# Second moments of attention keys from channel products on VectorE and GpSimd, in place of squared sums from TensorE and ScalarE

## The chip, the cores and the metric

The kernel runs on one core of one Trainium2 chip. The metric is the device time in microseconds (us) from launch to end; lower is better. Three runs of the kernel before gave 4068.22, 4074.77 and 4081.95 us, so the median is 4074.77. One more execution was taken with the hardware profiler.

The engines are called here as the profile calls them: PE is TensorE (matmuls), PEld its loading of weights, DVE is VectorE, ACT is ScalarE, POOL is GpSimd, SP is SyncE, which issues most of the DMAs. Everything is computed in float32.

## The reference, cut to what matters

The network has a convolution layer, then an attention layer, then a feed-forward layer on the upper half of the tokens. The images are 4 x 256 channels x 56 x 56, so the attention sees 4 batches of N = 3136 tokens of 256 channels, with 8 heads of 32 channels. Only the attention is touched by the change:

```python
NUM_HEADS = 8
C_SHIFT = 5.0
qkv = x @ qkv_w.T + qkv_b
q, k, v = (qkv[:, :, 0], qkv[:, :, 1], qkv[:, :, 2])
scores = jnp.einsum('bnhd,bmhd->bhnm', q, k) * scale
t = jnp.square(scores + C_SHIFT)
attn = t / jnp.sum(t, axis=-1, keepdims=True)
out = jnp.einsum('bhnm,bmhd->bnhd', attn, v)
return out @ proj_w.T + proj_b
```

The weight of a key is the square of a shifted score, so it is a polynomial of degree two in the key. The sum over all keys can therefore be taken before the queries are known. What is needed of the keys of one head is the sum over tokens of v times each product of two channels k_i k_j (the second moments), of v times k_i, and of v alone, and for the divisor the same sums without v.

## The kernel before, in words

The program has three parts, one after the other: `conv_layer`, the attention in `attn_ffn_layers`, and the feed-forward layer at the end of `attn_ffn_layers`.

**How the attention is staged.** For each of the 4 images b, `keys(b, 0)` and `keys(b, 1)` (line 1000) gather the sums over keys for the two groups of four heads; after each, `coefficients(b, g)` (line 1089) turns the sums into the weights of the queries' features; then `queries(b)` (line 1179) goes over the tokens again in 7 chunks of 448. I call the two runs of `keys` of an image its key stages. The loop that sets this order is at lines 1438 to 1448.

**One token tile of a key stage.** There are NT = 25 tiles of 128 tokens (the last has 64). For tile m, in the order in which they are written:

- `features(m)` (line 1035): four matmuls (one for each head, 32 rows each) multiply the transposed keys `kT` by the constant `pairs`, whose columns each have ones at two channels. The result `pf`, 496 columns a head, is k_i + k_j for all pairs i < j. ACT squares it into `phi` (line 1048), which has two buffers; DVE sets column 496 to one (line 1046).
- `add(m - 1)` (line 1051): four matmuls add v times `phi` of the tile before into the PSUM tile `accs`; four small ones add v times the squares and the keys into `accq`; one of 128 by 129 columns adds keys times keys and keys times one, for the divisor, to `accq` as well.
- `tokens(m + 3)` (line 1009): two matmuls give keys and values `pv` of a later tile with tokens on partitions; DVE adds the bias (line 1021) to the keys in `ls` and to `v`, and squares the keys (line 1025).
- `channels(m + 2)` (line 1027): PE transposes the keys into `pk`, and DVE copies them to `kT`.

So every tile of the keys passes through PE twice before it is summed: once to be transposed, once to make the sums of pairs.

**From squared sums to products.** (k_i + k_j)^2 holds the product that is wanted and two squares. `coefficients` takes this apart. It copies the sums to SBUF, transposes them in five blocks (`pt`, `pr`), and eight matmuls with the constants `pair_to` and `rest_to` (`pc`) and six further ones (`pd`) give `cf`, the weights of the queries' pairs, and `cd`, the weights of their squares and of the queries themselves. `gram` and `line` are for the divisor.

**Work beside.** Everything that isn't in these loops is a generator in the list `later`; each `yield` of a key or query stage calls `aside()` (line 1427), which takes every one of them a step further. Four of them matter for the prediction: `divide` and `tokens_out` finish the last chunks of an image while the key stage of the next one runs (`po` on PE; `uw` and `tk` on POOL, lines 1317 and 1318); `select(b)` then finds the upper half of an image's tokens (`hit` on DVE, `pn` on PE), and at its end scatters 28 blocks of rows to the DRAM tile `us` by indirect DMAs from POOL (line 1421), two for each step; and `project` makes the queries of a chunk, with their squares on POOL (line 1152). `select` of image b runs in the key stages of image b + 1; that of the last image runs in the feed-forward layer.

**What sets the order.** The framework places semaphores and may reorder instructions of an engine. `InOrder` (line 841) wraps an engine so that its instructions keep the order in which they are written. In `attn_ffn_layers` DVE, PE, ACT and SP are wrapped (line 897). POOL isn't; its instructions there are issued through `nc.gpsimd`.

**Buffers.** `phi` has two, `ls` five (`NKV`), `v` five, `kT` four; the small PSUM tiles (`pv`, `pk`, and those of the work beside) share two of tag `sm`.

Of the kernel before, what the change touches and what calls it, by code (L numbers as in the profile page):

```python
# [7 lines left out]
F32 = mybir.dt.float32  # L8
I32 = mybir.dt.int32
AF = mybir.ActivationFunctionType  # L10
ALU = mybir.AluOpType
# [843 lines left out]
LS = 2 * DH + 1  # L855
# [3 lines left out]
def attn_ffn_layers(  # L859
    ctx: ExitStack, tc: tile.TileContext, d, xs: bass.AP, ln0: bass.AP, us, out: bass.AP  # L860
):

# [34 lines left out]
    ve, te, se, sy = (  # L897
        InOrder(tc, e) for e in (nc.vector, nc.tensor, nc.scalar, nc.sync)
# [15 lines left out]
    pair_to = const.tile([P, FB + 1, P], F32, name="pair_to")  # L914
    nc.sync.dma_start(pair_to, d["pair_to"])
    rest_to = const.tile([LS, NF + 2 * P], F32, name="rest_to")
# [26 lines left out]
    for i in range(NKV):  # L943
        ls = const.tile([P, 2 * P + 1], F32, name=f"ls{i}")
        nc.gpsimd.memset(ls[:, 2 * P :], 1.0)
        lss.append(ls)
# [53 lines left out]
    def keys(b, g):  # L1000

        xn = xns[b]
        accs = accp.tile([P, 512], F32, tag="acc", name=f"accs_{b}_{g}")
        accq = accp.tile([P, 512], F32, tag="acc", name=f"accq_{b}_{g}")
        held["sums", b, g] = accs, accq
        vs, kts = {}, {}
        size = lambda m: min(P, HW - m * P)

        def tokens(m):

            mn = size(m)
            ls = lss[m % NKV]
            v = vs[m] = kp.tile([P, P], F32, tag="v", name=f"v_{b}_{g}_{m}", bufs=5)
            p = sm.tile([P, 512], F32, tag="sm", name=f"pv_{b}_{g}_{m}")
            for c in range(2):
                te.matmul(
                    p[:mn, : 2 * P], xn[:, c, m * P : m * P + mn],
                    wqkv[:, c, C:].rearrange("p (i o) -> p i o", i=2)[:, :, g * P : (g + 1) * P],
                    start=c == 0, stop=c == 1,
                )  # L1020
            for i, to in enumerate((ls[:mn, P : 2 * P], v[:mn])):
                ve.tensor_tensor(
                    to, p[:mn, i * P : (i + 1) * P], kvb[:mn, i, g * P : (g + 1) * P], ALU.add
                )
            ve.tensor_tensor(ls[:mn, :P], ls[:mn, P : 2 * P], ls[:mn, P : 2 * P], ALU.mult)

        def channels(m):

            mn = size(m)
            p = sm.tile([P, 512], F32, tag="sm", name=f"pk_{b}_{g}_{m}")  # L1030
            te.transpose(p[:, :mn], lss[m % NKV][:mn, P : 2 * P], ident[:mn, :mn])
            kts[m] = kp.tile([P, P], F32, tag="kT", name=f"kT_{b}_{g}_{m}", bufs=4)
            ve.tensor_copy(kts[m][:, :mn], p[:, :mn])

        def features(m):
            mn = size(m)
            kT = kts.pop(m)
            p = [
                mm.tile([P, 2, 512], F32, tag="mm", name=f"pf{i}_{b}_{g}_{m}") for i in range(2)
            ]  # L1040
            for h, r in enumerate(QUARTERS):
                te.matmul(
                    p[h // 2][:mn, h % 2, :NP], kT[r, :mn], pairs[r, :NP], start=True, stop=True
                )
            phi = php.tile([P, 4, 512], F32, tag="phi", name=f"phi_{b}_{g}_{m}")
            ve.memset(phi[:mn, :, NP : NP + 1], 1.0)
            for i in range(2):
                se.activation(phi[:mn, 2 * i : 2 * i + 2, :NP], p[i][:mn, :, :NP], AF.Square)
            return phi

        def add(m, phi):
            mn = size(m)
            v, ls = vs.pop(m), lss[m % NKV]
            first, last = m == 0, m == NT - 1
            for h, r in enumerate(QUARTERS):
                te.matmul(accs[r, : NP + 1], v[:mn, r], phi[:mn, h, : NP + 1], start=first, stop=last)
            both = ls[:mn, : 2 * P].rearrange("p (i h e) -> p i h e", i=2, e=DH)
            for h, r in enumerate(QUARTERS):
                te.matmul(
                    accq[r, : 2 * DH].rearrange("p (i e) -> p i e", i=2), v[:mn, r],  # L1060
                    both[:, :, h], start=first, stop=last, skip_group_check=True,
                )

            te.matmul(
                accq[:, P : 2 * P + 1], ls[:mn, P : 2 * P], ls[:mn, P:], start=False, stop=last,
                skip_group_check=True,
            )

        tokens(0)
        tokens(1)  # L1070
        yield
        channels(0)
        tokens(2)
        yield
        channels(1)
        waiting = None
        for m in range(NT):
            phi = features(m)
            if waiting:
                add(*waiting)  # L1080
            waiting = m, phi
            if m + 3 < NT:
                tokens(m + 3)
            if m + 2 < NT:
                channels(m + 2)
            yield
        add(*waiting)

    def coefficients(b, g):
# [3 lines left out]
        st = stp.tile([P, NF + P], F32, tag="st", name=f"st_{at}")  # L1093
        ve.tensor_copy(st[:, :NP], accs[:, :NP])
        ve.tensor_copy(st[:, NF : NF + 2 * DH], accq[:, : 2 * DH])
        ve.tensor_copy(st[:, NF + 2 * DH : NF + LS], accs[:, NP : NP + 1])
        gram = cp.tile([P, P], F32, tag="gram", name=f"gram_{at}")
        ve.tensor_tensor(gram, accq[:, P : 2 * P], own.rearrange("p h e -> p (h e)"), ALU.mult)
        line = cp.tile([P, 1], F32, tag="line", name=f"line_{at}")
        ve.tensor_scalar(line, accq[:, 2 * P : 2 * P + 1], 2 * CSHIFT, None, ALU.mult)  # L1100
        held["form", b, g] = gram, line
        yield
        sums = stp.tile([P, FB + 1, P], F32, tag="sums", name=f"sums_{at}")
        kns = (P, P, P, NP - 3 * P)
        p = sm.tile([P, FB, P], F32, tag="sm", name=f"pt_{at}")
        for k, kn in enumerate(kns):
            te.transpose(p[:kn, k], st[:, k * P : k * P + kn], ident)
        ve.tensor_copy(sums[:, :3], p[:, :3])
        ve.tensor_copy(sums[: kns[3], 3], p[: kns[3], 3])
        yield  # L1110
        p = sm.tile([P, 512], F32, tag="sm", name=f"pr_{at}")
        te.transpose(p[:LS, :P], st[:, NF : NF + LS], ident)
        ve.tensor_copy(sums[:LS, FB], p[:LS, :P])
        yield
        cf = cp.tile([P, FB, 4, DH], F32, tag="cf", name=f"cf_{at}")
        p = sm.tile([P, FB, P], F32, tag="sm", name=f"pc_{at}")
        for k, kn in enumerate(kns):
            te.matmul(p[:, k], pair_to[:kn, FB], sums[:kn, k], start=True, stop=False)
            te.matmul(
                p[:, k], rest_to[:, k * P : (k + 1) * P], sums[:LS, FB], start=False, stop=True  # L1120
            )
        ve.tensor_copy(cf.rearrange("p k h e -> p k (h e)"), p)
        yield
        p = sm.tile([P, 2, P], F32, tag="sm", name=f"pd_{at}")
        for k, kn in enumerate(kns):
            te.matmul(p[:, 0], pair_to[:kn, k], sums[:kn, k], start=k == 0, stop=False)
        te.matmul(p[:, 0], rest_to[:, NF : NF + P], sums[:LS, FB], start=False, stop=True)
        te.matmul(p[:, 1], rest_to[:, NF + P :], sums[:LS, FB], start=True, stop=True)
# [9 lines left out]
    def project(b, q):  # L1138
# [5 lines left out]
        for g in range(2):  # L1144
# [7 lines left out]
            nc.gpsimd.tensor_tensor(q2[:, g], qT[:, g], qT[:, g], ALU.mult)  # L1152
# [26 lines left out]
    def queries(b):  # L1179
# [3 lines left out]
        def add(q, g, k, phi):  # L1183
# [4 lines left out]
            for h, r in enumerate(QUARTERS):  # L1188
                te.matmul(
                    acc[r, :CH], cf[:, k, h], phi[:, h, :CH], start=k == 0, stop=False,  # L1190
                    skip_group_check=True,
                )
# [76 lines left out]
    def tokens_out(b, q, both):  # L1269
# [47 lines left out]
        nc.gpsimd.tensor_tensor(uw, u, wr.to_broadcast([TB, 4, C]), ALU.mult)  # L1317
        nc.gpsimd.tensor_tensor(tk, tk, u, ALU.add)
# [11 lines left out]
    def select(b):  # L1330
# [89 lines left out]
        for m in range(NTB):  # L1420
            nc.gpsimd.indirect_dma_start(  # L1421
                us[b], bass.IndirectOffsetOnAxis(ap=to[:, m : m + 1], axis=0), rows[:, m], None
            )
            if m % 2:
                yield
# [79 lines left out]
    def second(i):  # L1505
# [10 lines left out]
        for m in range(0, k, 2):  # L1516
# [10 lines left out]
            for j in range(2):  # L1527
# [4 lines left out]
                nc.gpsimd.indirect_dma_start(  # L1532
# [34 lines left out]
def pair_constants():  # L1567
# [4 lines left out]
    i, j = np.triu_indices(DH, 1)  # L1572
    n = np.arange(NP)
    eye = np.eye(DH, dtype=np.float32)
# [3 lines left out]
    to_sq = np.zeros((NF, DH), np.float32)  # L1578
    to_sq[n, i] = to_sq[n, j] = -0.5
    pair_to = np.zeros((FB + 1, P, P), np.float32)  # L1580
    pair_to[:FB] = np.tile(to_sq.reshape(FB, P, DH), (1, 1, 4))
    pair_to[FB] = 0.5 * np.eye(P, dtype=np.float32)
    rest_to = np.zeros((LS, NF + 2 * P), np.float32)
    rest_to[:DH, :NF] = -0.5 * pairs
    rest_to[2 * DH, NP] = CSHIFT * CSHIFT
    rest_to[:DH, NF : NF + P] = np.tile(0.5 + DH / 2 * eye, (1, 4))
    rest_to[DH : 2 * DH, NF + P :] = np.tile(2 * CSHIFT * eye, (1, 4))
# [6 lines left out]
        "pair_to": pair_to.transpose(1, 0, 2),  # L1594
# [113 lines left out]
```

## Time and profile before

The profiled execution took 4070.11 us; its span, from the first to the last instruction, is 4068.2 us, and the mean granted clock of PE 0.974.

| stretch (us from the start of the span) | us | PE busy | DVE busy | ACT busy | POOL busy |
|---|---|---|---|---|---|
| key stages of image 0, 1872 to 2066 | 194 | 188.6 | 50.4 | 94.2 | 0 |
| queries of image 0, 2066 to 2316 | 250 | 234.0 | 105.0 | 117.0 | 38.0 |
| key stages of image 1, 2316 to 2520 | 204 | 193.5 | 75.4 | 93.9 | 31.1 |
| queries of image 1, 2520 to 2776 | 256 | 239.9 | 106.6 | 117.0 | 42.8 |
| key stages of image 2, 2776 to 2978 | 202 | 191.4 | 74.8 | 92.6 | 31.1 |
| key stages of image 3, 3232 to 3434 | 202 | 191.1 | 74.2 | 91.5 | 31.2 |
| feed-forward layer, 3645 to 4068 | 423 | 396.8 | 113.4 | 77.1 | 89.2 |

The table is read from the windows view. A stage is bound by the engine whose busy time comes near to its length, if that engine's gaps aren't waits for another. The busy times of the engines are sums of records; an instruction that waits for something inside counts as busy.

In the timeline, a line gives start, time to the end of the last of the merged instructions, engine, line of the program (L849 is the wrapper of `InOrder`, so the tiles' names tell more), operation, what it writes and reads, and how many were merged. Every float32 matmul has two records. In brackets stands the idle time of the engine before it, and what ended it. The ends of matmuls are modelled; their starts tell more, so durations of steps on PE are best read from start to start.

### The profile page before, as it was taken

What the parts mean: (1) busy time and instruction counts of PE and PEld (TensorE: products, weight loads), DVE (VectorE), ACT (ScalarE), POOL (GpSimd) and SP (SyncE); (2) the same over time, 40 slices, a digit from 0 to 9 for tenths busy, and PEclk for the clock granted to TensorE, in tenths of its full rate; (3) what the DMA queues carried; (4) which work ended last, traced back from release to release, by engine and by line L of the source; (5) the groups of instructions that cost most, each with busy time, mean ns of one, the idle gap of its engine ahead of it and who ended that gap; (6) DMA issues with size and microseconds to landing.
All of it is one profiled execution on the core that took longest, in us unless ns stands there. A gap on an engine that the chain in (4) does not pass through costs nothing.

```text
span 4068.2 us, 62879 instructions
## 1 busy us (share of the span) xinstructions
PE 3774.7 (93%) x23956; PEld 1715.7 (42%) x23956; DVE 2343.7 (58%) x4112; ACT 2137.6 (53%) x3837; POOL 1805.0 (44%) x856
## 2 busy tenths in 40 slices
PE   3989998999799989997999999999999999999998
PEld 1333333333233333333544444334444444436776
DVE  2688988898789889993224442344324442333321
ACT  2767766776577657753454444444444444542111
POOL 1678878898688889982002102111112102111231
PEclk7999999999899999998999999999999999999999
DMA  3666566664666465552002201121012201121120
GB/s 99 145 154 147 120 150 152 147 135 99 146 140 139 99 132 122 122 110 67 1 20 63 56 10 33 51 59 38 16 38 62 56 6 33 38 65 50 42 61 25
DMA packets 337377, 330.44 MB, mean 81 GB/s; under 512 B 68459, under 2 KB 327555, under 8 KB 337076
## 3 DMA queue, kind: packets, MB, share of 16 engines
q1 hardware_dynamic: 322282, 302.90, 32.3%
q0 software_dynamic: 8064, 19.48, 1.6%
q10 hardware_dynamic: 6730, 4.05, 0.4%
q8 instruction: 189, 3.10, 0.3%
q14 instruction: 112, 0.92, 0.1%
HBM read 257.15 MB, written 68.69 MB: 80 GB/s over the span
## 4 chain that ended last, share of the span: by engine, by line
PE 79%; DVE 9%; DMA 5%; issue 3%; POOL 1%; ACT 1%; SPq 1%; ACTq 0%; DVEq 0%; POOLq 0%
PE acc L849 18%; PE p L849 16%; PE pf L849 5%; PE pg L849 5%; PE accs L849 5%; PE py L849 4%; PE pv L849 4%; PE ph L849 4%; PE po L849 4%; DVE pr L849 3%; PE z L849 3%; PE accq L849 3%; PE pq L849 2%; DMA xc<-x3d 1%; DVE st L849 1%
## 5 line engine op out<-in xcount | busy, mean ns | idle before, releaser
L849 POOL TENSOR_TENSOR pr<-xc,lg 128x1792 f32<-128x1792 f32 x280 | 1035.1, 3706 | 270.2 <-ACT lg L849 104.4
L849 PE MATMUL acc<-pr,same 128*32 128x448 f32 (+1 forms) x5824 | 676.2, 557 | 69.6 <-DVE pr L849 56.8
L849 PE MATMUL p<-y,cw 128*128 128x400 f32 (+5 forms) x1568 | 679.2, 537 | 2.4 <-ACT y L849 1.5
L849 ACT ACTIVATE ph<-pg,unit 128x896 f32<-128x896 f32 x448 | 426.3, 1003 | 420.7 <-PE pg L849 376.6
L849 ACT ACTIVATE phi<-pf 128x992 f32<-128x992 f32 (+1 forms) x400 | 377.0, 994 | 449.5 <-issue 390.8
L849 DVE TENSOR_TENSOR pr<-xc,exp 128x1792 f32<-128x1792 f32 x280 | 559.2, 1998 | 52.0 <-DMA xc<-x3d 31.2
L849 ACT ACTIVATE y<-p,tb,bn2s 128x200 f32<-128x200 f32 (+1 forms) x728 | 341.8, 519 | 223.5 <-PE p L849 219.4
L849 PEld LDWEIGHTS p<-y,cw 128*128 128x128 f32 (+1 forms) x1568 | 265.9, 191 | 400.0 <-issue 204.4
L849 DVE TENSOR_TENSOR pr<-xw,exp 128x1792 f32<-128x1792 f32 x168 | 338.5, 2016 | 41.8 <-DMA xw<-x3d 17.0
L1317 POOL TENSOR_TENSOR uw<-rows,awr 112x1024 f32<-112x1024 f32 x28 | 66.0, 2356 | 613.5 <-DVE rows L849 613.5
L849 POOL TENSOR_TENSOR y<-a,ac 128x896 f32<-128x896 f32 x168 | 277.7, 1654 | 125.9 <-DMA ac<-x3d 95.3
L849 PEld LDWEIGHTS acc<-pr,same 128*32 128x32 f32 (+1 forms) x5824 | 144.5, 110 | 425.2 <-issue 239.5
L1421 POOL DMA_INDIRECT us<-rows,to x112 | 105.8, 944 | 489.2 <-DVE phi L849 287.4
L849 DVE TENSOR_TENSOR ls<-pv,kvb 128x128 f32<-128x128 f32 (+1 forms) x200 | 58.2, 291 | 448.9 <-PE pv L849 448.9
L849 PE MATMUL pg<-qT,pairs 32*128 32x448 f32 x1792 | 281.3, 587 | 8.7 <-ACT ph L849 8.5
L1152 POOL TENSOR_TENSOR q<-qT 128x448 f32<-128x448 f32 x56 | 58.3, 1044 | 508.4 <-DVE qT L849 465.6
L849 PE MATMUL pv<-wqkv,xn 128*128 128x256 f32 (+1 forms) x800 | 215.0, 395 | 27.2 <-DMA xn<-ln 18.7
L849 PE MATMUL pf<-pairs,kT 32*128 32x496 f32 (+1 forms) x1600 | 233.9, 638 | 0.0
L849 ACT ACTIVATE lg<-p,par 128x448 f32<-128x448 f32 x392 | 233.0, 594 | 1.4 <-PE p L849 1.3
L849 ACT ACTIVATE h<-ph,apar 128x448 f32<-128x448 f32 (+1 forms) x128 | 68.2, 583 | 288.0 <-PE ph L849 287.9
L849 PE MATMUL acc<-ph,cf 128*32 128x448 f32 x1792 | 214.8, 551 | 0.0
L849 ACT ACTIVATE lg<-lg 128x1120 f32<-128x1120 f32 x168 | 163.9, 1007 | 95.5 <-DVE lg L849 95.0
(238 smaller groups left out, 5742.2 us busy)
## 6 DMA issues: line engine op xcount, KB each, us to landing
xw<-x3d SPq DMA_DIRECT2D x224, 248.0 KB
xq<-in_x SPq DMA_DIRECT2D x47, 448.0 KB
xc<-x3d SPq DMA_DIRECT2D x54, 248.0 KB
xc<-x3d SPq DMA_DIRECT2D x54, 247.0 KB
xc<-x3d SPq DMA_DIRECT2D x54, 246.0 KB
xc<-x3d SPq DMA_DIRECT2D x54, 245.0 KB
xr<-in_x SPq DMA_DIRECT2D x224, 56.0 KB
xs<-xr SPq DMA_DIRECT2D x224, 56.0 KB
```

The costliest lines, as they stand in the source:

```text
L849: return lambda *a, **k: self.tc.keep_in_program_order(of(*a, **k))
L1152: nc.gpsimd.tensor_tensor(q2[:, g], qT[:, g], qT[:, g], ALU.mult)
L1317: nc.gpsimd.tensor_tensor(uw, u, wr.to_broadcast([TB, 4, C]), ALU.mult)
L1421: nc.gpsimd.indirect_dma_start(us[b], bass.IndirectOffsetOnAxis(ap=to[:, m : m + 1], axis=0), rows[:, m], None)
```

## The change

The sums of pairs and their squares are replaced by products. With keys laid out with tokens on partitions and channels along the row, the product of channel i and channel (i + l) mod 32 for all i is one product of the row with the row shifted by l. Lag 0 gives the squares, lags 1 to 15 give 32 pairs each, and lag 16 gives the last 16 pairs. To make shifted reads simple, `ls` holds each head's keys twice in succession.

For each token tile:

- The transposition `pk`, the copy to `kT`, the four matmuls `pf`, ACT's two squares, and DVE's square and memset are no longer there; `channels` is gone.
- DVE writes the keys to `ls` twice with one instruction, from PSUM.
- DVE makes lags 0 to 9 (`VE_LAGS`), 1280 elements a partition, and POOL lags 10 to 15, 768 elements, both from `ls` to `phi`; POOL makes lag 16, 64 elements, within `ls`.
- `accs` takes 512 columns instead of 497. The small matmuls `accq` take 81 columns instead of 64, and the one of 129 columns becomes one of 65 columns for each head.

In `coefficients` the sums are the products already, so the eight matmuls `pc` and the copy of their result fall away, with one step; `pair_to` and `rest_to` become smaller (`to_sq`, `rest_to`). The queries' features stay as they are, in another order of pairs; their last block takes 113 rows instead of 128.

POOL is wrapped in `InOrder` as well (`gp`), and its operations and indirect DMAs in this function go through it.

```diff
-LS = 2 * DH + 1
+KNS = (P, P, P, NP + 1 - 3 * P)
+HALF = DH // 2
+
+LS = HALF + 2 * DH + 1
+VE_LAGS = 10
...
-    ve, te, se, sy = (
-        InOrder(tc, e) for e in (nc.vector, nc.tensor, nc.scalar, nc.sync)
+    ve, te, se, sy, gp = (
+        InOrder(tc, e) for e in (nc.vector, nc.tensor, nc.scalar, nc.sync, nc.gpsimd)
     )
...
-            for i, to in enumerate((ls[:mn, P : 2 * P], v[:mn])):
-                ve.tensor_tensor(
-                    to, p[:mn, i * P : (i + 1) * P], kvb[:mn, i, g * P : (g + 1) * P], ALU.add
-                )
-            ve.tensor_tensor(ls[:mn, :P], ls[:mn, P : 2 * P], ls[:mn, P : 2 * P], ALU.mult)
-
-        def channels(m):
+            of = slice(g * P, (g + 1) * P)
+            twice = lambda a: (
+                a.rearrange("p (h e) -> p h e", e=DH).unsqueeze(2).to_broadcast([mn, 4, 2, DH])
+            )
+            ve.tensor_tensor(
+                ls[:mn, :, HALF : HALF + 2 * DH].rearrange("p h (i e) -> p h i e", i=2),
+                twice(p[:mn, :P]), twice(kvb[:mn, 0, of]), ALU.add,
+            )
+            ve.tensor_tensor(v[:mn], p[:mn, P : 2 * P], kvb[:mn, 1, of], ALU.add)
+
+        def features(m):
 
             mn = size(m)
-            p = sm.tile([P, 512], F32, tag="sm", name=f"pk_{b}_{g}_{m}")
-            te.transpose(p[:, :mn], lss[m % NKV][:mn, P : 2 * P], ident[:mn, :mn])
-            kts[m] = kp.tile([P, P], F32, tag="kT", name=f"kT_{b}_{g}_{m}", bufs=4)
-            ve.tensor_copy(kts[m][:, :mn], p[:, :mn])
-
-        def features(m):
-            mn = size(m)
-            kT = kts.pop(m)
-            p = [
-                mm.tile([P, 2, 512], F32, tag="mm", name=f"pf{i}_{b}_{g}_{m}") for i in range(2)
-            ]
-            for h, r in enumerate(QUARTERS):
-                te.matmul(
-                    p[h // 2][:mn, h % 2, :NP], kT[r, :mn], pairs[r, :NP], start=True, stop=True
-                )
-            phi = php.tile([P, 4, 512], F32, tag="phi", name=f"phi_{b}_{g}_{m}")
-            ve.memset(phi[:mn, :, NP : NP + 1], 1.0)
-            for i in range(2):
-                se.activation(phi[:mn, 2 * i : 2 * i + 2, :NP], p[i][:mn, :, :NP], AF.Square)
+            ls = lss[m % NKV]
+            k = ls[:mn, :, HALF : HALF + DH]
+
+            def further(n, lags):
+
+                a = ls[:mn, :, HALF + n : HALF + n + DH]
+                return bass.AP(a.tensor, a.offset, [*a.ap[:2], [1, lags], a.ap[2]])
+
+            phi = php.tile([P, 4, NF], F32, tag="phi", name=f"phi_{b}_{g}_{m}")
+            for e, n, lags in ((ve, 0, VE_LAGS), (gp, VE_LAGS, HALF - VE_LAGS)):
+                e.tensor_tensor(
+                    phi[:mn, :, n * DH : (n + lags) * DH].rearrange("p h (l e) -> p h l e", e=DH),
+                    k.unsqueeze(2).to_broadcast([mn, 4, lags, DH]), further(n, lags), ALU.mult,
+                )
+            gp.tensor_tensor(
+                ls[:mn, :, :HALF], k[:, :, :HALF], k[:, :, HALF:], ALU.mult
+            )
             return phi
...
-                te.matmul(accs[r, : NP + 1], v[:mn, r], phi[:mn, h, : NP + 1], start=first, stop=last)
+                te.matmul(accs[r], v[:mn, r], phi[:mn, h], start=first, stop=last)
             for h, r in enumerate(QUARTERS):
                 te.matmul(
...
-            te.matmul(
-                accq[:, P : 2 * P + 1], ls[:mn, P : 2 * P], ls[:mn, P:], start=False, stop=last,
-                skip_group_check=True,
-            )
+                    accq[r, :LS], v[:mn, r], ls[:mn, h], start=first, stop=last,
+                    skip_group_check=True,
+                )
+
+            for h, r in enumerate(QUARTERS):
+                k = ls[:mn, h, HALF:]
+                te.matmul(
+                    accq[r, P : P + LS - HALF], k[:, :DH], k, start=False, stop=last,
+                    skip_group_check=True,
+                )
...
-        cf = cp.tile([P, FB, 4, DH], F32, tag="cf", name=f"cf_{at}")
-        p = sm.tile([P, FB, P], F32, tag="sm", name=f"pc_{at}")
-        for k, kn in enumerate(kns):
-            te.matmul(p[:, k], pair_to[:kn, FB], sums[:kn, k], start=True, stop=False)
-            te.matmul(
-                p[:, k], rest_to[:, k * P : (k + 1) * P], sums[:LS, FB], start=False, stop=True
-            )
-        ve.tensor_copy(cf.rearrange("p k h e -> p k (h e)"), p)
...
-            nc.gpsimd.tensor_tensor(q2[:, g], qT[:, g], qT[:, g], ALU.mult)
+            gp.tensor_tensor(q2[:, g], qT[:, g], qT[:, g], ALU.mult)
...
-        nc.gpsimd.tensor_tensor(uw, u, wr.to_broadcast([TB, 4, C]), ALU.mult)
-        nc.gpsimd.tensor_tensor(tk, tk, u, ALU.add)
+        gp.tensor_tensor(uw, u, wr.to_broadcast([TB, 4, C]), ALU.mult)
+        gp.tensor_tensor(tk, tk, u, ALU.add)
...
-            nc.gpsimd.indirect_dma_start(
+            gp.indirect_dma_start(
                 us[b], bass.IndirectOffsetOnAxis(ap=to[:, m : m + 1], axis=0), rows[:, m], None
             )
```

## The prediction, made before the change was run

> **What bounds the kernel now.** I read the page first (chain, groups), then the timelines of the attention's key stages, then the timelines of POOL and DVE for what the change gives them.
>
> ```profile
> PE 79%; DVE 9%; DMA 5%; issue 3%; POOL 1%; ACT 1%; SPq 1%; ACTq 0%; DVEq 0%; POOLq 0%
> PE acc L849 18%; PE p L849 16%; PE pf L849 5%; PE pg L849 5%; PE accs L849 5%; PE py L849 4%; PE pv L849 4%; PE ph L849 4%; PE po L849 4%; DVE pr L849 3%; PE z L849 3%; PE accq L849 3%; PE pq L849 2%; DMA xc<-x3d 1%; DVE st L849 1%
> ```
> TensorE sets the end. `pf`, `accs`, `accq` and `pv` belong to the change: eight key stages (4 images, 2 groups) of 25 token tiles each, 200 tiles. One tile in the timeline of PE:
>
> ```profile
> 1929.46 1.04 PE L849 MATMUL accs<-phi,v 128*32 128x497 f32 x8
> 1930.32 0.29 PE L849 MATMUL accq<-ls,v 128*32 128x64 f32 x8
> 1930.54 0.49 PE L849 MATMUL accq<-ls 128*128 128x129 f32 x2
> 1930.87 1.03 PE L849 MATMUL pv<-wqkv,xn 128*128 128x256 f32 x4
> 1931.73 0.27 PE L849 MATMUL pk<-aident,ls 128*128 128x128 f32 x1
> 1931.93 1.11 PE L849 MATMUL pf<-pairs,kT 32*128 32x496 f32 x8
> 1932.98 1.04 PE L849 MATMUL accs<-phi,v 128*32 128x497 f32 x8
> ```
> From one `accs` to the next is 3.52 us with no gap: 0.86 `accs`, 0.22 and 0.33 `accq`, 0.86 `pv`, 0.20 `pk`, 1.05 `pf`. The windows view gives PE 76.00 of 76.00 us busy there, DVE 19.2, ACT 40.4, POOL 0. So 200 tiles are 704 us, PE-bound, and work taken from PE counts until another engine is late.
>
> **Does the shared access of DVE and POOL bite?** The change gives both long products with both inputs in SBUF. The timeline shows what happens when two such instructions meet:
>
> ```profile
> 2319.92 2.37 POOL L1317 TENSOR_TENSOR uw<-rows,awr 112x1024 f32<-112x1024 f32 x1 [29.67 <-DVE rows L849]
> 2321.11 0.29 DVE L849 TENSOR_TENSOR ls<-pv,kvb 128x128 f32<-128x128 f32 x1 [1.10 <-PE pv L849]
> 2321.51 0.93 DVE L849 TENSOR_TENSOR ls<-ls 128x128 f32<-128x128 f32 x1
> 2322.25 2.42 POOL L1318 TENSOR_TENSOR tk<-tk,rows 112x1024 f32<-112x1024 f32 x1
> 2325.03 0.28 DVE L849 TENSOR_TENSOR ls<-ls 128x128 f32<-128x128 f32 x1
> ```
> `ls<-ls` takes 0.28 us alone and 0.93 beside `uw`: it ends just after `uw` does, and before `tk` is under way in earnest. `ls<-pv,kvb`, with one input in PSUM, isn't held. The reverse shows too: POOL's `q<-qT` takes 0.93 us, and 1.24 when DVE's `av<-av,rec` is running.
>
> **And POOL's queue:**
>
> ```profile
> 2455.55 1.10 POOL L1421 DMA_INDIRECT us<-rows,to  x1 [95.77 <-DVE phi L849]
> 2458.55 0.94 POOL L1421 DMA_INDIRECT us<-rows,to  x1 [1.90 <-DMA us<-rows,to]
> 2461.42 0.94 POOL L1421 DMA_INDIRECT us<-rows,to  x1 [1.92 <-DMA us<-rows,to]
> ```
> The 28 row scatters of an image each wait at the head of POOL's queue for the one before to land: 2.85 us apiece, 80 us in all (2455.6 to 2534.5), inside the key stages of the next image. Today nothing that PE needs stands behind them.
>
> **What the Trainium skill says.** "SBUF — State Buffer", section "Who interferes with whom": a DVE instruction with two SBUF inputs contends with a GpSimd one that reads SBUF, and the second to issue blocks fully. The 0.93 against 0.28 us agrees, both ways round. "GPSIMD Engine Reference", section 3.1: a two-input elementwise operation is about half as fast as on DVE; the trace has 2.07 ns an element (`pr`, 1792 in 3.706 us) against 1.12 (1.998). "TensorEngine Tiling (Array Packing)", "Key Properties": a change of tiling mode drains the array; `pf` to `accs` takes 1.05 us where 497 columns in the same mode take 0.86, which agrees.
>
> **The change, part by part.**
>
> (1) PE per tile. `pk` (0.20) and `pf` (1.05) go. `accs` grows from 497 to 512 columns: 0.89. The column-group `accq` grows from 64 to 81: about 0.25. The 128x129 product becomes four column-group ones of 65 columns: 0.22, as `accq` today. `pv` stays at 0.86; one mode change, 0.15. Sum 2.37: PE could save 1.15 us a tile.
>
> (2) DVE per tile. The copy of kT, the square and the memset go. `ls` becomes one 256-element add from PSUM (0.28+0.13=0.41, pitch 0.34), `v` keeps its pitch of 0.20. New: a 1280-element product. `xn` (896) takes 1.08, `av` (448) 0.616; extended that is 1.48, of which about 1.40 holds the shared access (an operation after `av` starts 0.57 after it, so some 0.05 to 0.1 overlap). Sum about 1.95, under PE's 2.37. ACT's squares (1.89) go; nothing waits for ACT there any more.
>
> (3) POOL per tile. New: a 768-element product and a 64-element one, both SBUF. Rows of the trace lie between 2.03 (`q` back to back, 0.91) and 2.3 ns an element (`uw`): 1.57 to 1.77, I take 1.70. The small one isn't shown; at least its elements (0.13), at most 0.4; I take 0.2.
>
> (4) The cycle of a plain tile. The access passes from POOL's product to DVE's to POOL's small one: 1.70+1.40+0.20=3.30, longer than PE's 2.37, with DVE's two adds hidden beside POOL's product. Gain 3.52-3.30=0.22, times 200: **-44**. With the ends of (3), 3.1 to 3.6, this is -84 to +16.
>
> (5) The scatters. With the new order kept on POOL, two of them stand between one tile's products and the next: 14 tiles in each of three images (19 tiles are left when they begin, so all 14 fall in). In a period the products (1.9) run while the second scatter lands; then comes 0.94 issue, 1.90 wait, 0.94 issue: 5.7, and 6.05 if DVE's product is in the way at POOL's start. Behind the waiting scatter stand the next products, behind these `accs` of PE. I take 5.9: 42 times (5.9-3.3): **+109**. Only one tile of `phi` can be ahead (two buffers), so nothing cushions this.
>
> (6) `uw` and `tk` (2.3 each) fall twice in each of three key stages; they were free, now they stand in the access cycle: 6 times 4.6, **+28**.
>
> (7) The token output's matmuls `po` stretch a tile to 6.91 today (2331.67 to 2338.58), 3.39 more, six times. With PE at 2.37+2.8=5.2 they cost 1.9 over the cycle: **-9**. The selection's `hit` on DVE (0.60, two SBUF inputs) costs 0.9 today (4.42 against 3.52) through `pn` on PE, and about 0.85 then, through the access that it takes: 0.
>
> (8) Coefficients: eight `pc` matmuls (1.8 to 2.0 us) and the 0.69 copy go, one small copy comes. Between two groups `accs` starts 11.4 us after the last `accq` (1967.08 to 1978.46); without kT, `pf` and `pc` about 8, so -3.5 four times; before the queries -2.3 four times: **-23**. The first tile waits for constants (chain: `rest_to` 6.97 us); smaller ones give **-1**. Queries use the same shapes except 113 rows instead of 128: 0. In the feed-forward stage the scatters of the last image now stay in order with the output's; PE isn't waiting for either (fetches have two parts, 53 us, of lead): 0, at worst +10.
>
> Sum -44+109+28-9-23-1=**+60**. The profiled execution took 4070.1 (span 4068.2): 4130. The median of the runs shown is 4.7 above it, so **4135**.
>
> **Rivals.**
> - B, a longer cycle: POOL's 32-element runs, or an order forced between the two writers of `phi`, make it 3.7. For: no POOL row shown has runs that short. Against: runs of 56 (`pr`) cost no more than flat ones. The 158 tiles without scatters cost 0.4 more each, +63: 4198.
> - C, faster: the access doesn't serialise these two products (place: plain tiles; price: PE's 2.37 instead of 3.3). Then 158 tiles save another 0.93, -147, and `uw`, `tk` cost half: 3975. It decides against me once the plain tile falls below about 2.9 (158 times 0.4 is the whole +60). Against it: the 0.93 above.
> - D, nearly nothing: cycle 3.1 and scatters 5.5, that is -40 and -17: 4080, and down to 4060 with a little more overlap.
> - E, the products aren't held behind scatters: -109: 4026. Against: one queue, and the trace's waits at its head.
>
> **Chances.** Mine 0.50 (4085 to 4185), B 0.20, C 0.12, D 0.12, E 0.06. A measurement tells about 0.3% (12 us) from nothing. Faster than that: C, E and a third of D, 0.22; same: about half of D and a little of mine, 0.09; slower 0.69. Range 4015 to 4230: it leaves out C and B's tail. Mine alone is 4085 to 4185.
>
> **What would show it.** In the timeline of the changed kernel: plain tiles 3.3 us apart with gaps on PE before `accs` released by POOL's or DVE's `phi`; DVE's product lasting up to 3 us where it waits for POOL (or POOL's longer than 1.8); tiles beside scatters 5.7 to 6; `accs` waiting for POOL. Wrong if PE runs at 2.4 us a tile, if the products keep 1.5 and 1.7 us while they overlap, or if tiles beside scatters are as quick as others.

## The result, and the profile after

Over four runs each, the changed kernel takes 4229.47 us (4224.68 to 4231.91) and the kernel before 4078.36 us: 1.0373 times as long, 95% interval 1.035 to 1.0396, or some 151 us more. The forecast was 4135: slower, inside the range, but less than half of what came. The profiled span grew by 161.9 us, from 4068.2 to 4230.1.

Where it went is read from the timeline of PE, by cutting the span at the starts of the first and the last line of `accs` of each image:

| us | before | after |
|---|---|---|
| start to the first `accs` | 1883.7 | 1888.5 |
| key stages of image 0 | 178.4 | 160.6 |
| of image 1 | 199.7 | 258.5 |
| of image 2 | 199.9 | 253.6 |
| of image 3 | 200.3 | 252.2 |
| the three stretches between them | 769.6 | 765.2 |
| last `accs` to the end | 636.6 | 651.6 |

The same code gains 17.8 us in image 0 and loses 52 to 59 in each other image. The loss is made by what runs beside the keys there.

The page's groups of the changed kernel, first the new products and who waits for them (busy us and mean ns, then the idle time of the engine before them):

```profile
L849 PE MATMUL accs<-phi,v 128*32 128x512 f32 (+1 forms) x1600 | 272.7, 759 | 298.8 <-POOL phi L849 185.1
L849 POOL TENSOR_TENSOR phi<-ls 128x768 f32<-128x768 f32 (+1 forms) x200 | 400.7, 2004 | 177.2 <-DVE ls L849 97.2
L849 DVE TENSOR_TENSOR phi<-ls 128x1280 f32<-128x1280 f32 (+1 forms) x200 | 439.7, 2202 | 7.4 <-PE accs L849 7.4
L849 POOL TENSOR_TENSOR ls<-ls 128x64 f32<-128x64 f32 (+1 forms) x200 | 208.0, 1040 | 0.0
```

PE, which had hardly a gap in these stages, now stands still for 298.8 us before `accs`. The product on DVE has a mean of 2.20 us; its minimum, by the view of the tile `phi`, is 1.47. POOL's small product has a mean of 1.04 us, and is 0.33 where it meets nothing. Such durations hold waiting.

A plain tile (image 0), in the timeline of the changed kernel:

```profile
1922.27 1.06 PE L849 MATMUL accs<-phi,v 128*32 128x512 f32 x8 [0.84 <-DVE phi L849]
1922.27 1.71 POOL L849 TENSOR_TENSOR phi<-ls 128x768 f32<-128x768 f32 x1
...
1922.58 2.75 DVE L849 TENSOR_TENSOR phi<-ls 128x1280 f32<-128x1280 f32 x1
...
1923.94 1.57 POOL L849 TENSOR_TENSOR ls<-ls 128x64 f32<-128x64 f32 x1
...
1925.47 1.06 PE L849 MATMUL accs<-phi,v 128*32 128x512 f32 x8 [0.83 <-DVE phi L849]
```

DVE starts its product 0.3 us after POOL's, and ends at 1925.33: 1.35 us after POOL's end (1923.98), about what its own work takes. POOL's small product starts at 1923.94 and ends when DVE's has ended. The three follow each other in 3.20 us.

A tile beside the scatters (image 1) in the same kernel:

```profile
2457.24 1.93 PE L849 MATMUL accs<-phi,v 128*32 128x512 f32 x8 [1.81 <-POOL phi L849]
...
2458.89 0.97 POOL L849 DMA_INDIRECT us<-rows,to  x1 [0.16 <-issue]
...
2459.59 2.08 PE L849 MATMUL pv<-wqkv,xn 128*128 128x256 f32 x4
2461.75 0.94 POOL L849 DMA_INDIRECT us<-rows,to  x1 [1.89 <-PE pv L849]
2461.77 0.42 DVE L849 TENSOR_TENSOR ls<-pv,kvb 128x256 f32<-128x256 f32 x1 [3.23 <-PE pv L849]
2462.11 0.28 DVE L849 TENSOR_TENSOR v<-pv,kvb 128x128 f32<-128x128 f32 x1
2462.31 3.47 DVE L849 TENSOR_TENSOR phi<-ls 128x1280 f32<-128x1280 f32 x1
2462.71 1.71 POOL L849 TENSOR_TENSOR phi<-ls 128x768 f32<-128x768 f32 x1
2464.37 1.59 POOL L849 TENSOR_TENSOR ls<-ls 128x64 f32<-128x64 f32 x1
2464.47 1.93 PE L849 MATMUL accs<-phi,v 128*32 128x512 f32 x8 [2.81 <-POOL phi L849]
```

From `accs` to `accs` is 7.23 us, all of it on POOL: a scatter, the wait for it to land (the second starts 2.86 after the first), the second scatter, POOL's product, and a small product of 1.59. DVE's product was sent off at 2462.31, while the second scatter was being issued, and ends at 2465.78: it ran behind POOL's product, and POOL's small product behind it. The bracket `<-PE pv` on the second scatter names the event that was last by the profile; 2.86 is also the pitch of scatters in the profile of before, where nothing else is near.

The product isn't always held so. In another tile (image 2) it is sent off 0.09 us after the start of the second scatter:

```profile
2999.71 0.94 POOL L849 DMA_INDIRECT us<-rows,to  x1 [1.95 <-DMA us<-rows,to]
2999.80 1.48 DVE L849 TENSOR_TENSOR phi<-ls 128x1280 f32<-128x1280 f32 x1
3000.67 2.17 POOL L849 TENSOR_TENSOR phi<-ls 128x768 f32<-128x768 f32 x1
```

Neither the product nor the scatter is lengthened here; POOL's product waits instead (2.17 for 1.71). In the whole trace the four products sent 0.09 to 0.28 us after the start of a scatter of 0.94 us take 1.48 each; the 15 sent 0.34 to 0.56 us after it take 3.47 to 3.69.

In the windows view of the changed kernel a column stands out that the prediction didn't look at, PE's granted clock (the last but two):

```profile
1890.00:1960.00 70.00, 50.44 (x592) 27.26 (x595) 66.88 (x65) 0.00 (x0) 70.00 (x43) 0.98 0.01 1
2307.00:2358.00 51.00, 30.47 (x288) 17.97 (x290) 36.85 (x60) 0.30 (x1) 37.20 (x22) 0.80 0.12 33
2362.00:2418.00 56.00, 40.59 (x375) 20.82 (x378) 48.18 (x86) 0.00 (x0) 37.62 (x27) 0.77 0.00 1
2456.00:2550.00 94.00, 53.74 (x364) 24.48 (x364) 43.43 (x41) 0.00 (x0) 65.19 (x52) 0.62 0.11 33
```

Beside the scatters the clock is 0.62, and `pv` and `accs` take 2.08 and 1.93 us in place of 1.13 and 1.06. "TensorE: Matmul & The Clock Gate", Part 1, ties the clock to how busy PE was just before, which agrees: PE has work for about a third of that tile (an estimate: 2.33 us, the length of a tile without gaps in the run with keys in PSUM below, of 7.23). Whether it costs time is another question.

### The profile page after: what moved, and what is told of

Its sections match the earlier page's. It is cut to its first block, busy times and chain, and to the rows that moved or that the text cites. A ratio compares the mean times of both kernels' runs of the same rounds, so it can differ in the third digit from the quotient of the medians.

```text
span 4230.1 us, 61388 instructions
## 1 busy us (share of the span) xinstructions
PE 3647.2 (86%) x23228; PEld 1652.8 (39%) x23228; DVE 2724.0 (64%) x3720; ACT 1762.9 (42%) x3437; POOL 2420.7 (57%) x1256
## 5 line engine op out<-in xcount | busy, mean ns | idle before, releaser
L849 PE MATMUL accs<-phi,v 128*32 128x512 f32 (+1 forms) x1600 | 272.7, 759 | 298.8 <-POOL phi L849 185.1
L849 POOL TENSOR_TENSOR phi<-ls 128x768 f32<-128x768 f32 (+1 forms) x200 | 400.7, 2004 | 177.2 <-DVE ls L849 97.2
L849 DVE TENSOR_TENSOR phi<-ls 128x1280 f32<-128x1280 f32 (+1 forms) x200 | 439.7, 2202 | 7.4 <-PE accs L849 7.4
L849 PE MATMUL pv<-wqkv,xn 128*128 128x256 f32 (+1 forms) x800 | 278.5, 484 | 18.2 <-DMA xn<-ln 16.8
L849 DVE TENSOR_TENSOR ls<-pv,kvb 128x256 f32<-128x256 f32 (+1 forms) x200 | 83.5, 417 | 261.0 <-PE pv L849 254.8
L849 PE MATMUL acc<-ph,cf 128*32 128x448 f32 (+1 forms) x1792 | 214.8, 551 | 0.0
L849 POOL TENSOR_TENSOR ls<-ls 128x64 f32<-128x64 f32 (+1 forms) x200 | 208.0, 1040 | 0.0
L849 ACT ACTIVATE y<-y 128x896 f32<-128x896 f32 x224 | 180.5, 806 | 61.7 <-POOL y L849 35.4
```

The source lines that it names most:

```text
L849: return lambda *a, **k: self.tc.keep_in_program_order(of(*a, **k))
```

## The experiments

Three theories. **Q**: POOL's kept order puts the scatters, and `uw` and `tk`, ahead of the products. **A**: the access that DVE and POOL share makes their instructions wait for each other. **C**: PE's clock falls in its waits, and slower matmuls lengthen the circle (the round of steps that each tile repeats). A and C were each held to explain why the scatter tile is 7.25 and not 5.9. In the table: the median and its ratio to the kernel before in the same session, then the stretches as above, from the profiled execution.

| kernel | us | ratio (95%) | image 0 | 1 | 2 | 3 | last `accs` to end |
|---|---|---|---|---|---|---|---|
| scatters later | 4106.16 | 1.0049 (1.0031 to 1.0067) | 160.6 | 202.4 | 201.7 | 207.9 | 660.3 |
| free order | 4078.21 | 0.9987 (0.9979 to 0.9996) | 161.8 | 209.2 | 208.0 | 206.0 | 638.6 |
| one scatter a tile | 4117.05 | 1.0096 (1.007 to 1.0123) | 160.6 | 218.3 | 218.6 | 218.8 | 637.8 |
| before, order kept | 4091.41 | 1.0032 (1.0019 to 1.0044) | 178.4 | 202.8 | 199.8 | 202.8 | 646.5 |
| all on DVE | 4061.3 | 0.9942 (0.9922 to 0.9961) | 145.2 | 188.6 | 188.1 | 187.1 | 667.5 |
| keys in PSUM | 4062.39 | 0.9945 (0.9924 to 0.9966) | 116.8 | 222.7 | 213.3 | 223.1 | 645.9 |
| filler matmuls | 4224.18 | 1.0353 (1.0338 to 1.0368) | 160.7 | 253.6 | 256.6 | 252.0 | 646.9 |
| PSUM, scatters later | 3948.58 | 0.9686 (0.9667 to 0.9704) | 116.8 | 161.8 | 162.6 | 162.0 | 660.7 |
| PSUM, free order | 3916.37 | 0.9597 (0.9583 to 0.9611) | 116.5 | 170.2 | 170.7 | 169.8 | 636.2 |
| the same, 12 shifts on DVE | 3920.19 | 0.9613 (0.9591 to 0.9635) | 121.8 | 168.9 | 169.4 | 168.2 | 637.0 |

**Scatters held back until the keys are done.** POOL's order stays kept.

```diff
         yield
+        while held.get("keys"):
+            yield
         for m in range(NTB):
             gp.indirect_dma_start(
...
+        held["keys"] = True
         for g in range(2):
             run(keys(b, g))
             later.append(coefficients(b, g))
             aside()
+        held["keys"] = False
```

> The changed kernel, but the 28 row scatters of an image wait until the key stages of the next image are over and run beside its queries. Theory Q (queue: the scatters stand ahead of the products in POOL's kept order): the 42 tiles beside scatters fall from 7.3 us to about 3.2, some 130 to 170 us less in all, of which up to 15 us an image may come back where the squares of the queries now stand behind scatters: 4060 to 4120. Theory A (shared access of DVE and POOL alone): the scatters hardly matter, 4200 to 4230. Theory C (PE's clock falls in its waits and slows the chain): without long waits the clock stays, so the same as Q; it is not told apart here.

The stages of images 1 to 3 fall from 255 to 204 us on average. Part comes back in the queries, whose squares (`q`, on POOL) now stand behind pairs of scatters, and in the feed-forward. PE's waits in this kernel, from the last `accs` to the end (total us, times, the longest):

```profile
PE ft L849 <- DMA frows<-us: 19.8, 2, 12.2
PE acc L849 <- POOL q L849: 11.1, 1, 11.1
```

**POOL's order left to the framework.** Everything else of the change stays.

```diff
+    gp = nc.gpsimd
     par = const.tile([P, len(COLS)], F32, name="apar")
```

> The changed kernel with POOL's order in the attention and the feed-forward layer left to the framework, as before the change; it puts one scatter beside a tile instead of two, and the other half beside the queries. Q: a tile beside scatters takes about 4.2 us (3.2 and one issue of 0.94, the landing hidden behind the products), key stages of images 1 to 3 some 40 us shorter each, the feed-forward layer 10 to 15 us shorter: 4080 to 4110. A: no change in the key stages, only the tail: 4210 to 4220. C: like Q.

The framework puts one scatter between the products of a tile rather than two. The kernel is then as fast as the one before, within what can be told. So Q's order costs about 151 us of the changed kernel (157 by the two ratios): the whole measured loss. That does not make A nothing, as the next runs show; the change would have been a gain without either.

**One scatter in each tile, order kept.**

```diff
-            if m % 2:
-                yield
+            yield
```

> The changed kernel with one scatter in each of the last tiles in place of two in each second half of them, everything else kept. In the profile of the changed kernel a tile with two scatters is 7.25 us, of which 2.86 lie between the starts of the two (the second waits until the first has landed). If what a scatter costs is its place in the circle, 0.96 of its own and that wait: with one in a tile the wait is over before the next is due, a tile is 3.3 + 0.96 and 0.2 to 0.4 for a held access, 4.4 to 4.7; per image about 24 tiles x 4.55 = 109 in place of 14 x 7.25 + 10 x 3.3 = 134, and 4 scatters beside the queries: 3 x -25 = about -75, 4145 to 4175. If each scatter costs the same wherever it stands (1.97 us: half of 7.25 - 3.3), no change: 4215 to 4235.

The tiles repeat at 4.40 and 4.41 us, inside the forecast of 4.4 to 4.7; the time falls further than forecast, as the last stretch lost its excess too (637.8 us). No scatter waits for a landing in these tiles. The 112 us against the changed kernel are the price of two scatters side by side in a kept queue: the second's wait holds up all that is behind it.

**The kernel before, with POOL's order kept and nothing else.** 
```diff
-    ve, te, se, sy = (
-        InOrder(tc, e) for e in (nc.vector, nc.tensor, nc.scalar, nc.sync)
+    ve, te, se, sy, gp = (
+        InOrder(tc, e) for e in (nc.vector, nc.tensor, nc.scalar, nc.sync, nc.gpsimd)
     )
...
-            nc.gpsimd.indirect_dma_start(
+            gp.indirect_dma_start(
```

(and so in the other four places of the attention and feed-forward).

> The kernel before, with GpSimd's instructions kept in the order of the program and nothing else of the change. Theory Q, put to the rest of the program: beside the attention's keys the kept order costs nothing here, since GpSimd has no product to hold back, and the scatters of the feed-forward's end cost what the changed kernel's stretch from the last accs on showed, 651 against 637 us: 4085 to 4095. If that stretch is late for another reason (its last selection running later because of the longer key stage), no change: 4070 to 4082.

Some 11 us slower (0.19 to 0.44%). The two profiled spans differ by 20.7 us; 9.9 of it is the last stretch, and the rest, spread over the stages and the stretches between them, was not taken apart. PE's waits in the last stretch, in the kernel before, and with the order kept:

```profile
PE ft L849 <- DMA frows<-us: 11.4, 1, 11.4
```

```profile
PE ft L849 <- DMA frows<-us: 20.1, 2, 11.4
```

The second wait, 9 us, is also in the changed kernel (two waits, 20.5 in all). The kept order alone makes it, beside no product at all.

**All 16 shifts and the small product on DVE**, so that no product of POOL is left in the key stages.

```diff
-VE_LAGS = 10
+VE_LAGS = HALF
...
-            for e, n, lags in ((ve, 0, VE_LAGS), (gp, VE_LAGS, HALF - VE_LAGS)):
+            for e, n, lags in ((ve, 0, VE_LAGS),):
...
-            gp.tensor_tensor(
+            ve.tensor_tensor(
                 ls[:mn, :, :HALF], k[:, :, :HALF], k[:, :, HALF:], ALU.mult
```

> The changed kernel with all 16 lags and the last product on DVE, none on POOL. DVE then has 2048 elements (2.2 us), two adds (0.54) and a small product (0.15) a tile: about 2.9 us, and no product stands behind a scatter or waits for POOL. Q and A both: key stages of 25 x 2 x 2.9 = 145 us and fills for image 0, 160 to 175 for the others with the selection's DVE work in line, 3900 to 3950. If instead C alone held (PE's clock), tiles would be bound by a slow PE at 4 us or more: 4050 or above.

A miss. The time lies in the range put down for C alone, but the tiles don't: none is bound by a slow PE. Scatter tiles take 2.87 us, as plain ones do, so scatters harm only what stands behind them on POOL. But DVE is the bound: from start to start 0.34 and 0.20 for the additions, 2.20 for the product, 0.14 for the small one. Selection's own work on DVE comes on top, and its tiles take 4.20 and 3.53, hardly better than before (4.42 and 3.52). With shorter tiles the scatters also outlast the stages: in the last stretch PE waits up to 19.2 us for a `q` behind them.

This run also tells what holds DVE's product in the changed kernel. Here no product stands behind the scatters:

```profile
2437.21 0.95 POOL L849 DMA_INDIRECT us<-rows,to  x1 [1.91 <-DMA us<-rows,to]
2437.94 2.27 DVE L849 TENSOR_TENSOR phi<-ls 128x2048 f32<-128x2048 f32 x1
```

The 23 products sent 0.57 to 0.75 us after the start of such a short scatter take 2.27 to 2.28, so the issue alone doesn't hold them. In the changed kernel it is POOL's product, next in the queue, that goes first; why it does, though DVE's product starts before it by the profile, is not shown.

**Keys in PSUM for DVE's product.** ACT, almost idle in these stages after the change, copies the keys to a PSUM tile, so that DVE's product has only one input in SBUF. POOL's work and order are unchanged.

```diff
+            pk = mm.tile([P, 2, 512], F32, tag="mm", name=f"pk_{b}_{g}_{m}")
+            kp4 = pk[:mn, 0, :P].rearrange("p (h e) -> p h e", e=DH)
+            se.activation(kp4, k, AF.Identity)
...
-                    k.unsqueeze(2).to_broadcast([mn, 4, lags, DH]), further(n, lags), ALU.mult,
+                    (kp4 if e is ve else k).unsqueeze(2).to_broadcast([mn, 4, lags, DH]),
+                    further(n, lags), ALU.mult,
```

> The changed kernel, but ACT copies each tile's keys to PSUM and DVE's product takes one input from there, so that it has only one SBUF input. A: DVE's and POOL's products overlap in full; DVE's stays at 1.5 us, the plain tile falls from 3.21 to about 2.4 us (PE), the key stages of image 0 from 161 to about 125 us; tiles beside scatters fall to 5.8; about 4020 to 4060. Q without A: plain tiles stay at 3.2, total above 4200. Q with A: the tiles beside scatters stay far above the plain ones, at 5.7 to 6.

This takes away A and nothing else. The time is just above the 4020 to 4060 put down for A: 167 us under the changed kernel (175 by the two ratios). A plain tile falls from 3.21 to 2.33 us, close to the 2.37 of part (1), and PE is without a gap; the windows view of image 0 in this run:

```profile
1950.00:2000.00 50.00, 50.00 (x601) 27.05 (x603) 42.94 (x65) 5.97 (x21) 42.15 (x42) 1.00 0.01 2
```

DVE's product never lasts longer than 1.49 us here, nor POOL's longer than 2.07 (5.40 and 4.75 in the changed kernel). A scatter tile of this run:

```profile
2436.05 1.94 PE L849 MATMUL accs<-phi,v 128*32 128x512 f32 x8 [2.75 <-POOL phi L849]
2436.43 0.97 POOL L849 DMA_INDIRECT us<-rows,to  x1 [0.17 <-issue]
...
2438.40 2.07 PE L849 MATMUL pv<-wqkv,xn 128*128 128x256 f32 x4
2439.33 0.94 POOL L849 DMA_INDIRECT us<-rows,to  x1 [1.92 <-DMA us<-rows,to]
2440.29 1.71 POOL L849 TENSOR_TENSOR phi<-ls 128x768 f32<-128x768 f32 x1
...
2441.12 1.48 DVE L849 TENSOR_TENSOR phi<-pk,ls 128x1280 f32<-128x1280 f32 x1
2441.95 0.33 POOL L849 TENSOR_TENSOR ls<-ls 128x64 f32<-128x64 f32 x1
2442.05 1.93 PE L849 MATMUL accs<-phi,v 128*32 128x512 f32 x8 [1.58 <-POOL phi L849]
```

6.00 us, with `pv` at half speed (2.07) all the same. The small product is 0.33 again: the missing 1.25 us were its wait for DVE's product. This already speaks against C.

**Filler matmuls that keep PE's clock up**, four behind the keys and values of each tile that has scatters; their result is thrown away.

```diff
+            if held.get("scatter"):
+                p = mm.tile([P, 2, 512], F32, tag="mm", name=f"pw_{b}_{g}_{m}")
+                for i in range(4):
+                    te.matmul(
+                        p[:, i % 2, :CH], ident, xn[:, i // 2, :CH], start=True, stop=True,
+                        skip_group_check=True,
+                    )
             yield
...
+        held["scatter"] = True
         for m in range(NTB):
...
+        held["scatter"] = False
```

> The changed kernel with four filler matmuls of 448 columns behind the keys and values of each tile in which scatters are under way; their result is thrown away. Theory C (with 26 of TensorE's 28 us idle gaps per tile its clock falls to 0.62, the keys' and values' matmuls take 2.08 us in place of 1.13, so the DVE product misses the idle stretch of GpSimd between the two scatters and is held behind the second scatter and GpSimd's product): with the clock kept near 1.0 the keys and values end about 1.9 us earlier against the second scatter, the DVE product is through before it, the small product is 0.33 us again, and the tile falls from 7.25 us to the 6.0 that the run with keys in PSUM has: 14 tiles x 3 images x 1.25 = about -52 us, 4165 to 4190. Theory A alone (the two engines' accesses exclude each other whatever the clock): no tile gets shorter, and the fillers cost nothing or up to 1 us a tile: 4225 to 4270.

(The gaps of "26 of TensorE's 28 us" are in no trace; the gap in the tile shown above is 2.81 us, before `accs`.) The windows view gives a clock of 0.98 beside the scatters, and the time is that of the changed kernel. A tile of this run:

```profile
2485.59 1.13 PE L849 MATMUL pv<-wqkv,xn 128*128 128x256 f32 x4
...
2487.37 1.48 DVE L849 TENSOR_TENSOR phi<-ls 128x1280 f32<-128x1280 f32 x1
2487.59 2.07 POOL L849 DMA_INDIRECT us<-rows,to  x1 [1.90 <-DVE v L849]
2489.68 1.71 POOL L849 TENSOR_TENSOR phi<-ls 128x768 f32<-128x768 f32 x1
2491.34 0.33 POOL L849 TENSOR_TENSOR ls<-ls 128x64 f32<-128x64 f32 x1
2491.45 1.07 PE L849 MATMUL accs<-phi,v 128*32 128x512 f32 x8 [1.72 <-POOL phi L849]
```

C is right in its first half: `pv` is quick again, DVE's product starts ahead of the second scatter, the small product is 0.33. But the second scatter now takes 2.07 us in place of 0.94: its issue waits for DVE's product, and ends 0.81 us after it; of the 36 scatters here that start beside a running product 35 end 0.81 to 0.84 us after it. The price moved from one waiter to another and the tile is 7.11. C falls, A stands: these scatter tiles pay about one turn of the shared access, whoever waits.

**Both causes taken away.** Keys in PSUM, with the scatters held back, and with POOL's order free (the two edits above, put together); then the last also with 12 shifts on DVE and 4 on POOL:

```diff
-VE_LAGS = 10
+VE_LAGS = 12
```

> Keys in PSUM for the DVE product, and the scatters held until the keys are done. If A and Q add: the run with keys in PSUM has key stages of 117 and 213 to 223 us, of which the scatter tiles are 15 x 6.0 = 90; at 2.33 us each they are 35, so three stages lose 55 us each; the run with later scatters gave back 10 to 13 us between stages and 9 at the end, some 35 in all. 4062 - 165 + 35 = 3932, taken 3900 to 3960. If PSUM only moved the loss elsewhere, so that the two overlap: 4000 to 4060.

> Keys in PSUM for the DVE product, and GpSimd's instructions left free of the kept order. The freed order interleaved one scatter per tile; GpSimd then has 0.96 + 1.72 + 0.33 = 3.0 us a tile against 2.33 without, for the 28 scatters of a stage. If A and Q add: stages of 117 and about 165 to 175 us, stage gaps and end as in the run with the freed order (254 and 639): 117 + 3 x 170 + 3 x 254 + 1888 + 639 = 3916, taken 3890 to 3945. If the free order had already taken most of what the shared accesses cost: 3990 to 4060.

> Keys in PSUM for the DVE product and GpSimd free of the kept order, with 12 channel shifts on DVE and 4 on GpSimd in place of 10 and 6. GpSimd's product goes from 1.72 to about 1.2 us, DVE's from 1.48 to about 1.76. In the run with 10 shifts a tile with a scatter was 3.15 (GpSimd bound: 0.97 + 1.72 + 0.33 and gaps) and a plain one 2.33 (TensorE bound); selection's tiles (2.6 and 3.47) have DVE on the path. Expected: scatter tiles 2.6, 14 x 3 x -0.5 = -21; selection's 16 tiles x 3 x +0.28 = +13; so 3895 to 3920 if both hold. If GpSimd was not what bounds those tiles: 3925 to 3940.

The first two came where the sum of A and Q puts them. PSUM with the free order is the fastest version found, 4% under the kernel before (0.9583 to 0.9611) and some 313 us under the changed kernel (316 by the two ratios), about the sum of what Q (151) and A (167) give singly. Its scatter tiles are 3.15 us. The third shortened those to 2.9, not to the 2.6 that was forecast, and gave it back in plain tiles and selection's: no gain.

## Why the prediction was right in direction and wrong in size

- **Part (4), the plain tile.** Right: 3.30 forecast, 3.21 measured, with the waits that were named. Image 0 has no work beside it and gains 17.8 us; 50 times 0.22 and one group change of 3.5 are 14.5. Keys in PSUM showed the cause by taking it away. Rivals B and C fall with this, since the one needed 3.7 and the other under 2.9. D needed scatter tiles of 5.5, and E none that wait for scatters; both fall with part (5).
- **Part (5), the scatter tiles: the step that failed.** That the products would stand behind the scatters was right; the term was too small. The tile was put at 5.7, "and 6.05 if DVE's product is in the way at POOL's start", taken 5.9; the 14 tiles average 7.25 in image 1 (2451.76 to 2553.21), 7.10 in image 2 and 7.06 in image 3. Over 5.9 that is 52 us of the excess. The circle without any shared access is 6.0, as keys in PSUM showed, so 0.3 of what was missing from 5.7 is the circle itself. The other 1.25 is the access, for which 0.35 was allowed at most. The prediction counted the access for product against product, and took a scatter as time on POOL's queue alone. In the trace a scatter that starts while DVE's product runs waits for the end of it (11 scatters, 1.46 to 2.23 for 0.94), and a product sent late in the issue comes behind POOL's next product (3.47 for 1.48). "SBUF — State Buffer", "Who interferes with whom", allows for this only in part: it has a DVE instruction with two SBUF inputs contend with POOL's reads, and infers that the making of descriptors needs only the write side. For the issue of this indirect scatter, which does wait, the measurement decides.
- **Part (6), `uw` and `tk`.** Too small as well. Each pair spoils two tiles: 15.34 and 15.66 us in image 1 where two plain tiles and 4.6 would be 11.2, so 8.6 an image more than the term had, some 26 in all (images 2 and 3 show the same pairs). Beside DVE's product `uw` takes 3.70, not 2.36, and DVE's product 4.22 and 5.39. With a free order the same stretches are 11.7 and 11.3, with keys in PSUM 12.8 and 12.4, with both 8.4 and 8.7.
- **Part (8), the feed-forward**, was 0, "at worst +10", because fetches had a lead. It is 15.0 in the profiled execution, of which the order kept alone gives 9.9. The lead covers a delay of the output's scatters, but not of the last image's rows that `ft` fetches. This term was named and priced too low.
- **The rest** held. Queries: three stretches between the stages are 4.4 us shorter in all, coefficients included. The start is 4.8 us later, where -1 was forecast; it was not looked into.

Terms (5) and (6) with the feed-forward explain 93 of the 102 us between the sum of +60 and the 161.9 of the profiled spans; the remainders of both signs were not taken apart.

## What to carry to other kernels

When a change gives an engine a product that another engine needs every few microseconds, go through all that is queued on it, and count a DMA issue as an instruction like others: it can wait for a product of the other engine, and its wait for an earlier landing holds everything behind it. Before two engines split a product over SBUF, see whether one operand can lie in PSUM; here a free engine's copy of 0.28 us bought 0.88 us a tile. A cause that is worth the whole loss when undone need not be the only one: here undoing either of two gave about the same, and both together twice that.

## What the runs showed of the hardware that was not expected

- A GpSimd indirect scatter that starts while a DVE product of two SBUF inputs runs waits for the end of it: 11 scatters of the changed kernel take 1.46 to 2.23 us in place of 0.94 to 0.97, and end 0.81 to 0.98 after the product. The reverse was not seen: with no GpSimd product behind the scatter, a DVE product sent during its issue keeps its 2.27 to 2.28; with one behind it, a DVE product sent 0.34 to 0.56 us after the scatter's start takes 3.47 to 3.69 in place of 1.48. With one input in PSUM the product takes at most 1.49, and no scatter more than 1.18.
- PE's granted clock was 0.62 over 94 us in which it was busy for 57% by its (slowed) records, and 0.98 in the same tiles with fillers. That alone changed the time by nothing that can be measured: ratios 1.0353 and 1.0373, with overlapping intervals. A slow clock in an engine that isn't the bound can be the effect of a loss, not its cause.
